# Mask products of an attention kernel on the PE array: eight tiles of 32 rows by 64 columns instead of four of 32 by 128

## The chip, the cores and the metric

The kernel runs on one core of a Trainium2 chip. The metric is the device time of one execution in microseconds (us), lower is better; a kernel's figure is the median over its runs. The profile is one further execution, recorded by the hardware profiler.

## The reference, cut to what matters

Eight sequences (`B = 8`) of 512 positions and 256 features pass through two layers. The first is a feed-forward expert layer whose weights are picked for each sequence by an index. The second is a conditioned transformer layer with 16 heads of 16 features. Only its attention is touched here:

```python
x = _L0_cond_ref(x, itok_B_0_7, ...)                 # gelu(x Wi + bi) Wo + bo + x, then a layernorm
# in the second layer:
scores = jnp.einsum('bhqd,bhkd->bhqk', q / math.sqrt(HEAD_DIM), k)
scores = scores + attention_bias                     # fside, (8, 16, 512, 512), 128 MB
scores = jnp.where(src_mask, -jnp.inf, scores.astype(jnp.float32))
probs = jax.nn.softmax(scores, axis=-1).astype(v.dtype)
ctx = jnp.einsum('bhqk,bhkd->bhqd', probs, v)
# then ctx Wo, a residual, a layernorm, a gelu feed-forward with 1024 hidden features, a residual
```

The mask is a matrix of (8, 1, 512, 512) truth values, the same for all heads.

## The kernel before

**Tiling of the attention.** A step `s` handles one sequence and one block of 32 queries (`QB = 32`), for all 16 heads and all 512 keys; there are 8 x 16 = 128 steps. Heads are held as four quads `u` (`NU = 4`), each on 32 partitions of the q and k tiles, in two halves `r` (`ND = 2`). The scores of a step fill four PSUM tiles, `banks[u]`, each 128 partitions (4 heads x 32 queries) by 512 keys in float32, [...]. There is one set of four, so a step cannot start until the step before has been read out of them.

**A step, engine by engine** (`attention_step`). SP issues the load of the bias block `f` (1 MB, L964) and, every second step, of the mask bytes (L971). POOL turns the mask bytes into bf16 values of 0 or -1e30 in `mh` (L980). PE runs `score`: first the mask products (L990), which copy the mask of 32 queries to the four heads of a bank with a matrix of ones and zeros, `sel`, and open the accumulation (`start=True`), then the score products (L996), which add q k. DVE adds the bias and takes the row maximum (`add`, L1008), POOL negates it (L1021), ACT takes the exponentials (L1029), DVE transposes them in blocks of 32 (L1042).

**Shapes on PE.** The contraction of both products runs over 32 rows. A mask product has a stationary operand of 32 x 128 in bf16 and streams 512 columns; there are 4 in a step, one for each bank. A score product has a stationary operand of 32 x 64 in float32; there are 8 in a step, for each bank the partitions 0 to 63 and 64 to 127. Each float32 product goes to the array in two passes, so the profile counts 16 for a step. Every pass has its own weight load (PEld in the profile).

**Every fourth step** `attend(z)` follows: probabilities times values in 256 products (L1084) with a tile of 64 rows by 32 columns, planned as four pieces of 64 products (`sums`), then 16 small products for the row sums (L1100), the division on DVE, and the output projection (L1124). The names of the other PE lines: L544 is the up projection of either feed-forward layer, L567 the down projection, L716 and L764 are the projections to q, k and v, L522 are transposes, and L918 is the up projection in the last sequence's tail.

**The order of the work** is written out by a planner, `Weave.run`. It holds for each operation an engine, an estimated cost, a key (when it is due) and its dependencies, steps through an estimated time, and emits the operations in that order; each engine then runs its queue strictly in the order emitted, with semaphores between engines. For PE the planner also keeps a stock of instruction words, `words`: an operation's count of instructions, taken from a stock of at most `AT_ONCE = 256.0` that refills at `PER_US = 64.0` a us. An operation whose words are not in stock yet is given a later start. A float32 product counts 4 words (two passes, each a weight load and a product), a bf16 one 2.

Of the kernel before, what the change touches and what calls it, by code (L numbers as in the profile page):

```python
# [12 lines left out]
BF16 = mybir.dt.bfloat16  # L13
# [6 lines left out]
P = 128  # L20
# [6 lines left out]
QB = 32  # L27
# [50 lines left out]
class Weave:  # L78
# [10 lines left out]
    def op(self, engine, cost, key, emit, deps=(), takes=(), uses=(), table=None, lands=0.0,  # L89
           words=0):  # L90
        o = Op()
        o.engine, o.cost, o.key, o.emit = engine, cost, key, emit
        o.takes, o.uses = tuple(takes), tuple(takes) + tuple(uses)
        o.table, o.lands, o.words, o.end, o.done = table, lands, words, None, False
        o.after, o.ready = [], 0.0
        deps = list(deps) + [h.taker for h in uses]
        deps = {id(d): d for d in deps}.values()
        o.waits = len(deps)
        for d in deps:
            d.after.append(o)  # L100
        for h in o.uses:
            h.left += 1
        for h in o.takes:
            h.taker = o
        self.ops.append(o)
        return o
# [79 lines left out]
def tile_expert_ffn_then_conditioned_layer(  # L186
# [36 lines left out]
    nc = tc.nc  # L223
# [4 lines left out]
    ND = D // P  # L228
    NF = FF // P
    NQ = S // QB  # L230
    NU = 4
# [12 lines left out]
    def const(shape, name, dtype=F32):  # L244
        return pool.tile(shape, dtype, name=name)
# [30 lines left out]
    banks = [psum.tile([P, S], F32, name=f"sc_{u}") for u in range(NU)]  # L276
# [22 lines left out]
    eye = cst[:, n_c : n_c + 32]  # L299
    own = cst[:, n_c + 32 : n_c + 64]  # L300

    sel = const([P, 4, QB], "sel", BF16)
    nc.vector.tensor_copy(sel, eye.unsqueeze(1).to_broadcast([P, 4, QB]))

    def tiled(row):
        return row.unsqueeze(1).to_broadcast([P, NT, D])
# [2 lines left out]
    def load(mb, key, emit, **kw):  # L309
        return op("SP", mb / 0.26, key, emit, lands=1.8, **kw)  # L310
# [385 lines left out]
    q_h, k_h, x1t_h, vb_h = ([s.new() for _ in range(B)] for s in (s_q, s_k, s_xt, s_vb))  # L696
# [258 lines left out]
    def attention_step(s):  # L955
        b, i = steps[s]
        z = s // NI
        f, mh, top = s_fs.new(), s_mh.new(), s_top.new()
        if s % NI == 0:
            t_h[z], den_h[z], dg_h[z] = s_t.new(), s_den.new(), s_dg.new()  # L960
        den, t = den_h[z], t_h[z]

        def load_f():
            nc.sync.dma_start(f.tile, fside[b, i].rearrange("h q u k -> (h q) u k"))  # L964

        if s % 2 == 0:
            m8 = before["m8"] = s_m8.new()

            def load_m():
                for h in range(4):  # L970
                    nc.sync.dma_start(  # L971
                        m8.tile[QB * h : QB * h + QB],
                        mask[b, 0, i * QB : (i + 2) * QB, :].rearrange("(i q) k -> q i k", i=2),
                    )

            before["lm"] = load(0.14, s - 2.5, load_m, takes=[m8])
        m8 = before["m8"]

        def convert():
            nc.gpsimd.tensor_scalar(  # L980
                mh.tile, m8.tile[:, s % 2, :].bitcast(U8), MASKED, 1.0, ALU.mult, ALU.mult
            )

        lf = load(1.05, s - 2.4, load_f, takes=[f])
        mc = op("POOL", 0.65, s - 0.7, convert, deps=[before["lm"]], takes=[mh], uses=[m8])

        def score():
            quads = [slice(QB * u, QB * u + QB) for u in range(NU)]
            for u in range(NU):
                nc.tensor.matmul(  # L990
                    banks[u], sel[quads[u]].rearrange("p a q -> p (a q)"), mh.tile[quads[u], :],
                    start=True, stop=False,
                )
            for u in range(NU):
                for r in range(ND):
                    nc.tensor.matmul(  # L996
                        banks[u][64 * r : 64 * r + 64, :], q_h[b].tile[quads[u], r, i, :],
                        k_h[b].tile[quads[u], r, :], start=False, stop=True,
                    )

        sc = op(
            "PE", 1.25, s, score, deps=[mc] + q_ops[b] + k_ops[b] + before.get("A", []),
            uses=[mh, q_h[b], k_h[b]], words=2 * NU + 4 * NU * ND,
        )
        adds = []
        for u in range(NU):
            def add(u=u):
                nc.vector.tensor_tensor_reduce(  # L1008
                    out=f.tile[:, u, :], in0=banks[u], in1=f.tile[:, u, :], scale=1.0,
                    scalar=-3.0e38, op0=ALU.add, op1=ALU.max, accum_out=top.tile[:, u : u + 1],  # L1010
                )

            adds.append(op(
                "DVE", 0.62, s + 0.3, add, deps=[sc, lf], takes=[top] if u == 0 else [],
                uses=[f] + ([top] if u else []),
            ))
        before["A"] = adds

        neg = op(
            "POOL", 0.25, s + 0.3,  # L1020
            lambda: nc.gpsimd.tensor_scalar(  # L1021
                top.tile, top.tile, -BIG, 1.0 / BIG, ALU.mult, ALU.mult
            ),
            deps=adds, uses=[top],
        )
        exps = []
        for u in range(NU):
            def exp(u=u):
                nc.scalar.activation(  # L1029
                    f.tile[:, u, :], f.tile[:, u, :], AF.Exp, bias=top.tile[:, u : u + 1],  # L1030
                    accum_out=den.tile[:, u, s % NI : s % NI + 1],
                )

            first = s % NI == 0 and u == 0
            exps.append(op(
                "ACT", 0.71, s + 1.0, exp, deps=[neg], takes=[den] if first else [],
                uses=[f, top] + ([] if first else [den]), table="exp",
            ))
        E_all.setdefault(z, []).extend(exps)
        for h in range(2):  # L1040
            def turn(h=h):
                nc.vector.transpose(  # L1042
                    t.tile[:, s % NI, 2 * h : 2 * h + 2, :], f.tile[:, 2 * h : 2 * h + 2, :]
                )

            first = s % NI == 0 and h == 0
            T_of.setdefault(z, []).append(op(
                "DVE", 1.23, s + 2.0, turn, deps=exps[2 * h : 2 * h + 2],
                takes=[t] if first else [], uses=[f] + ([] if first else [t]),
            ))  # L1050
        if s % NI == NI - 1:
            attend(z)
# [101 lines left out]
    for b in range(B):  # L1154
        for i in range(NQ):
            if i == 0:
                line_v = values(b)
            attention_step(b * NQ + i)
        nxt = expert_layer(b + 1) if b + 1 < B else ([], [], [])
        ff = feed_forward(b - 1) if b > 0 else ([], [], [])  # L1160
        line = nxt[0] + line_v + ff[0][:2] + nxt[1] + ff[0][2:] + merged(ff[1], nxt[2], 1) + ff[2]
        if b + 1 < B:
            line += projections(b + 1)
        place(line, NQ * b, NQ * (b + 1.0))
# [60 lines left out]
```

## Time and profile before

| | |
|---|---|
| runs of the kernel before | 1056.48, 1062.85, 1064.83 us; median 1062.85 us |
| the profiled execution | 1061.58 us |
| its span, first to last instruction | 1059.8 us (1.8 us lie around it) |
| mean granted PE clock | 0.956 |
| busy: PE, DVE, ACT, POOL | 976.5, 776.6, 681.9, 297.5 us |
| PE products; instructions of all engines | 13329; 32062 |

How to read it: busy time is the union of an engine's instructions. A row of a group gives source line, engine, operation, tiles written and read, shape, count, then busy us, mean ns of one, and the idle time of the engine just before, with what ended it. "issue" means that no semaphore that the profile shows was waited for. A timeline row gives the start in us from the span's start, the length of a merged run of instructions, and how many there were; the length of a run reaches to the end of its last instruction, which on PE overlaps the next one.

### The profile page before, as it was taken

The page shows a single profiled execution, that of the slowest core. Times are in us where ns is not written, and L with a number is a line of the kernel's source. Part 1 is how long each engine was busy: PE and PEld are TensorE (multiplying, and loading weights), DVE is VectorE, ACT ScalarE, POOL GpSimd, SP SyncE. Part 2 cuts the span into 40 slices and gives each one's busy share as a digit, 9 for nine tenths or more (in the row PEclk, how much of TensorE's full clock was granted, in tenths as well). Part 3 has the DMA queues.
Part 4 walks back from the last instruction along what each step waited for, and adds up shares of the span by engine and source line. Part 5 has one row for each costly group of instructions (what it writes and reads, how often), then busy time and mean ns, then how long its engine had stood idle before and what let it go on. Part 6 is the DMA issues. An engine that isn't in the chain of part 4 may idle for free. (4 is left out here: it accounts for less than half of the span.)

```text
span 1059.8 us, 32062 instructions
## 1 busy us (share of the span) xinstructions
PE 976.5 (92%) x13329; PEld 549.1 (52%) x13329; DVE 776.6 (73%) x1837; ACT 681.9 (64%) x1453; POOL 297.5 (28%) x380
## 2 busy tenths in 40 slices
PE   6988989889999998999999999999999999988887
PEld 2643436435546464464745555464645555435466
DVE  1229868877869876789777878789777876777771
ACT  3136684576686755877579585878579574677473
POOL 1241161243222333125232243125132242121110
PEclk9998879989999998999999999999999998899899
DMA  6965436545555544465555645466553434444500
GB/s 202 323 208 173 167 120 230 197 149 190 199 169 194 204 138 147 171 225 181 201 192 190 206 128 199 171 224 181 200 190 130 169 132 146 171 132 163 180 12 17
DMA packets 67591, 183.33 MB, mean 173 GB/s; under 512 B 8212, under 2 KB 46438, under 8 KB 51062
## 3 DMA queue, kind: packets, MB, share of 16 engines
q1 hardware_dynamic: 67158, 181.25, 49.8%
q8 instruction: 104, 1.70, 0.7%
q14 instruction: 41, 0.34, 0.1%
q10 hardware_dynamic: 288, 0.04, 0.0%
HBM read 177.05 MB, written 4.21 MB: 171 GB/s over the span
## 5 line engine op out<-in xcount | busy, mean ns | idle before, releaser
L1029 ACT ACTIVATE fs<-fs,top 128x512 f32<-128x512 f32 x512 | 363.5, 712 | 154.0 <-POOL top L1021 153.0
L1008 DVE CUSTOM_DVE_ANT_0 fs<-sc,fs 128x512 f32<-128x512 f32 x512 | 323.2, 679 | 112.5 <-POOL mh L980 55.5
L1042 DVE STREAM_TRANSPOSE t<-fs 128x1024 f32<-128x1024 f32 x256 | 306.6, 1224 | 55.6 <-PE d L1084 50.3
L1084 PE MATMUL d<-t,vb 64*32 64x128 f32 x8192 | 149.2, 284 | 35.7 <-issue 32.6
L1084 PEld LDWEIGHTS d<-t,vb 64*32 64x32 f32 x8192 | 123.2, 110 | 90.3 <-issue 74.4
L996 PE MATMUL sc<-k,q 32*64 32x512 f32 x2048 | 156.7, 659 | 3.4 <-issue 3.4
L1021 POOL TENSOR_SCALAR top<-top 128x4 f32<-128x4 f32 x128 | 25.7, 201 | 417.8 <-DVE top L1008 368.6
L980 POOL TENSOR_SCALAR mh<-m 128x512 bf16<-128x512 uint8 x128 | 79.1, 618 | 199.5 <-PE sc L990 146.1
L544 PE MATMUL d<-xt,wi 128*128 128x512 f32 x256 | 122.3, 619 | 0.0
L567 PE MATMUL d<-w_t,hid 128*128 128x256 f32 x512 | 119.3, 386 | 2.2 <-issue 2.2
L567 PE MATMUL d<-wo,hid 128*128 128x256 f32 x512 | 120.2, 387 | 0.0
L567 PEld LDWEIGHTS d<-wo,hid 128*128 128x128 f32 x512 | 96.0, 192 | 28.4 <-issue 13.9
L567 PEld LDWEIGHTS d<-w_t,hid 128*128 128x128 f32 x512 | 95.8, 191 | 28.8 <-issue 14.8
L544 PE MATMUL d<-xt,w_t 128*128 128x512 f32 x224 | 105.3, 616 | 0.0
L1029 ACT ACTIVATION_READ_ACCUMULATOR fs<-fs,top 128x1 f32 x512 | 96.1, 188 | 0.0
L990 PE MATMUL sc<-mh,sel 32*128 32x512 bf16 x512 | 71.7, 397 | 19.3 <-DVE top L1008 18.8
L544 PEld LDWEIGHTS d<-xt,wi 128*128 128x128 f32 x256 | 47.5, 195 | 65.1 <-issue 57.7
L647 ACT ACTIVATE hid<-d,bc 128x512 f32<-128x512 f32 x64 | 42.8, 686 | 49.3 <-PE d L544 49.0
L544 PEld LDWEIGHTS d<-xt,w_t 128*128 128x128 f32 x224 | 41.9, 195 | 62.9 <-issue 45.1
L1029 ACT ACT_TABLE_LOAD x50 | 64.2, 1283 | 0.9
L617 POOL TENSOR_TENSOR xn<-xn,rows 128x1024 f32<-128x1024 f32 x24 | 56.7, 2361 | 23.8 <-DMA rows<-in_L_cond_bo_dram 12.5
L996 PEld LDWEIGHTS sc<-k,q 32*64 32x64 f32 x2048 | 31.6, 136 | 50.1 <-issue 49.8
(101 smaller groups left out, 865.6 us busy)
## 6 DMA issues: line engine op xcount, KB each, us to landing
fs<-in_fside_Bx16xSxS_dram SPq DMA_DIRECT2D x128, 1024.0 KB
wi<-in_L_cond_Wi_dram SPq DMA_DIRECT2D x8, 1024.0 KB
wo<-in_L_cond_Wo_dram SPq DMA_DIRECT2D x8, 1024.0 KB
m<-in_mask_Bx1xSxS_bk_dram SPq DMA_DIRECT2D x256, 32.0 KB
xt<-in_x_turned_dram SPq DMA_DIRECT2D x8, 512.0 KB
xn<-in_x_dram SPq DMA_DIRECT2D x8, 512.0 KB
out_dram<-xn SPq DMA_DIRECT2D x32, 128.0 KB
w_t<-in_L_cond_W_dram SPq DMA_DIRECT2D x2, 1024.0 KB
```

What stands on the lines that cost most here:

```text
L544: nc.tensor.matmul(h.tile, wt[:, c, f * P : (f + 1) * P], src.tile[:, c, :], start=(c == 0), stop=(c == ND - 1),)
L567: nc.tensor.matmul(h.tile[:, :D], lhs(f), wt[:, f, :], start=(f == 0), stop=(f == n - 1))
L617: lambda: nc.gpsimd.tensor_tensor(xn[b].tile, xn[b].tile, tiled(row()), alu),
L647: lambda: nc.scalar.activation(hid.tile[:, f, :], h.tile, AF.Gelu, bias=bc[b].tile[:, f : f + 1]),
L980: nc.gpsimd.tensor_scalar(mh.tile, m8.tile[:, s % 2, :].bitcast(U8), MASKED, 1.0, ALU.mult, ALU.mult)
L990: nc.tensor.matmul(banks[u], sel[quads[u]].rearrange("p a q -> p (a q)"), mh.tile[quads[u], :], start=True, stop=False,)
L996: nc.tensor.matmul(banks[u][64 * r : 64 * r + 64, :], q_h[b].tile[quads[u], r, i, :], k_h[b].tile[quads[u], r, :], start=False, stop=True,)
L1008: nc.vector.tensor_tensor_reduce(out=f.tile[:, u, :], in0=banks[u], in1=f.tile[:, u, :], scale=1.0, scalar=-3.0e38, op0=ALU.add, op1=ALU.m ...
L1021: lambda: nc.gpsimd.tensor_scalar(top.tile, top.tile, -BIG, 1.0 / BIG, ALU.mult, ALU.mult),
L1029: nc.scalar.activation(f.tile[:, u, :], f.tile[:, u, :], AF.Exp, bias=top.tile[:, u : u + 1], accum_out=den.tile[:, u, s % NI : s % NI + 1],)
L1042: nc.vector.transpose(t.tile[:, s % NI, 2 * h : 2 * h + 2, :], f.tile[:, 2 * h : 2 * h + 2, :])
L1084: nc.tensor.matmul(pc[r].tile[QB * u : QB * u + QB, :P], vb_h[b].tile[half, j, u, :], t.tile[half, :, u, QB * j : QB * j + QB], start=(j = ...
```

## The change

The mask products of a bank are issued as two products with 64 columns, one for each half `r` of the bank's partitions, in place of one with 128. Tile rows, tile columns and output partitions are then those of the score products that follow. `sel` is cut to 64 columns, and `words` is counted anew: 8 x 2 + 8 x 4 = 48 for a step, where it was 4 x 2 + 8 x 4 = 40. The planner's cost of the operation stays 1.25.

```diff
-    sel = const([P, 4, QB], "sel", BF16)
-    nc.vector.tensor_copy(sel, eye.unsqueeze(1).to_broadcast([P, 4, QB]))
+    sel = const([P, 2, QB], "sel", BF16)
+    nc.vector.tensor_copy(sel, eye.unsqueeze(1).to_broadcast([P, 2, QB]))
...
             for u in range(NU):
-                nc.tensor.matmul(
-                    banks[u], sel[quads[u]].rearrange("p a q -> p (a q)"), mh.tile[quads[u], :],
-                    start=True, stop=False,
-                )
+                for r in range(ND):
+                    nc.tensor.matmul(
+                        banks[u][64 * r : 64 * r + 64, :],
+                        sel[quads[u]].rearrange("p a q -> p (a q)"),
+                        mh.tile[quads[u], :], start=True, stop=False,
+                    )
...
             "PE", 1.25, s, score, deps=[mc] + q_ops[b] + k_ops[b] + before.get("A", []),
-            uses=[mh, q_h[b], k_h[b]], words=2 * NU + 4 * NU * ND,
+            uses=[mh, q_h[b], k_h[b]], words=6 * NU * ND,
```

## The prediction

> **What bounds the kernel now.** I read the page's busy table first, then the stretches, then PE's waits, then one step in the timeline. The page:
>
> ```profile
> PE 976.5 (92%) x13329; PEld 549.1 (52%) x13329; DVE 776.6 (73%) x1837; ACT 681.9 (64%) x1453; POOL 297.5 (28%) x380
> ```
>
> Two of seven equal stretches of 128 us (columns: length; PE, PEld, DVE, ACT, POOL busy us; clock; DMA share; GB/s):
>
> ```profile
> 461.00:589.00 128.00, 124.42 (x1741) 71.40 (x1741) 103.99 (x246) 91.15 (x196) 38.88 (x50) 1.00 0.54 186
> ...
> 845.00:973.00 128.00, 115.26 (x1623) 59.92 (x1622) 93.69 (x216) 85.17 (x181) 34.31 (x46) 0.92 0.42 146
> ```
>
> PE is busy 90 to 97% of every stretch between 77 and 973 us; DVE, the next, 73 to 81%. So time on PE is the time of the kernel, wherever PE isn't held by another. The largest of its waits, without two for the first inputs (9.3 and 4.1 us) and one for `hn` (3.0 us):
>
> ```profile
> PE d L1084 <- issue: 32.6, 22, 3.8
> PE sc L990 <- DVE top L1008: 18.8, 31, 3.2
> ...
> PE sc L996 <- issue: 3.4, 2, 2.4
> PE d L1084 <- DVE bc L636: 3.1, 3, 1.0
> ...
> PE d L567 <- issue: 2.2, 1, 2.2
> ```
>
> Two things hold PE. First, 38.2 us in 25 waits on "issue", all but three in the dense L1084 products. Going through the records one by one, the places lie 256 PE instructions, or multiples of it, apart: PE runs out of fetched instructions. Second, 18.8 us in which a mask product waits for DVE to empty its bank; these fall in 16 of the 128 steps.
>
> Now one step, PE's timeline:
>
> ```profile
> 504.44 0.55 PE L1084 MATMUL d<-t,vb 64*32 64x128 f32 x20
> 504.92 0.40 PE L990 MATMUL sc<-mh,sel 32*128 32x512 bf16 x4
> 505.25 1.11 PE L996 MATMUL sc<-k,q 32*64 32x512 f32 x16
> 506.29 0.34 PE L1084 MATMUL d<-t,vb 64*32 64x128 f32 x8
> ```
>
> Masks to scores takes 0.325 us, scores to the next line 1.044 us: these are also the medians over all steps (101 and 107 of the 128 lie within 0.016 us). Five float32 products of the full array just before show what a change of tile costs:
>
> ```profile
> 499.31 2.31 PE L544 MATMUL d<-xt,w_t 128*128 128x512 f32 x5
> 501.55 0.40 PE L1084 MATMUL d<-t,vb 64*32 64x128 f32 x2
> ```
>
> Their starts lie 0.427 us apart; 501.55 - 499.31 = 2.24 = 5 x 0.427 + 0.10. The 0.10 appears at each change of tile shape (L996 to L567: 0.517 from the last start, 0.090 over; L567 to L990: 0.312, 0.099 over 0.213), and not between L544 and L567, same shape (0.429).
>
> [...] The float32 loads agree: 102, 127 and 186 ns for the first of 32, 64 and 128 columns, some 0.8 ns a column. [...] The mask's load of 128 columns shows 90 ns, below the 32-column one, so it is fast now [...]. [...] The trace has the blocks (104 packets, 1.70 MB on queue q8) [...].
>
> **The change part by part.** *PE, one step.* Now, split so that it adds up:
> - masks 0.325 = starts of four spread over 0.010, one bf16 pass 0.213 (half of 0.427), drain and the fast load 0.102.
> - scores 1.044 = first weight load 0.053, two passes 2 x 0.427, starts of eight spread over 0.047, drain 0.090. The second passes' loads are hidden: they stand in the records under the first passes, and the second pass starts 0.480 = 0.427 + 0.053 after the first.
>
> Together 1.369 us. After, the mask is a third pass of the same eight tiles: weight load 0.053 [...], 0.213, 2 x 0.427, twice 0.007 handing over (last start of one pass to first start of the next is 0.434 now), 0.047 of spread, drain 0.090: 1.271. Saved 0.098, taken as 0.10. That rests on the drain between masks and scores going, and on the score weights loading under the masks.
>
> Bounds for the unseen:
> - The mask's load is still fast (0.013, an estimate from 90 against 102 ns at 32 columns): saved 0.138.
> - The score weights can't load under bf16 passes: saved 0.045.
> - The drain stays, since bf16 to float32 also drains (the trace has no other change of type to tell it by): masks 0.053 + 0.213 + 0.047 + 0.090 = 0.403 for 0.325: lost 0.078.
>
> *What counts on the path.* 128 steps, less those where another limit takes the gain. Of the 25 fetch waits, 13 follow a 256-instruction block that holds a whole step; there the block merely waits longer for its instructions. In the 16 steps with a DVE wait I count half: the adds that mask waits for themselves start after the scores of the step before, which come earlier too, as long as DVE isn't behind. 128 - 13 - 8 = 107; 107 x 0.10 = 10.7 us. What is late next at the other steps is PE's own following work (L567, L544, L1084), ready in 92% of the time.
>
> *Instructions.* 4 more products and 4 more loads a step, 1024 in all: four more blocks on 104. At 38.2 us for 104, +1.5 us. Issue itself is hidden: eight loads and products start 0.0067 us apart, in the 0.047 above. A mask product with its wait has the same things queued behind it as before.
>
> *The planner.* `words` 48 for 40 moves starts. Comparing the two orders: 35 of some 600 runs of equal PE work differ; about once a sequence from the third on, a mask-and-score operation stands one or two L567 halves earlier, once the transposes of `hn` are interleaved with `sums`, and in the tail L567 and `sums` alternate. DVE follows in 35 places (adds before transposes), ACT in 27, POOL in 5 with the same instructions. On SP the same loads are issued, in 17 places three `fs` loads in a row or a `rows` load earlier; `fs` has five buffers and DMA is busy 42 to 54%, so I take that as hidden; if not, it costs about one wait like the DVE ones, 1 us a sequence. Earlier masks can meet a full bank (a wait of 0.6 to 1 us, as in the DVE row) but also start DVE earlier. I take 0, bounds -4 and +6.
>
> The block boundaries also fall elsewhere. Counting the new order in 256s with the durations above, blocks that would run in under 4.5 us are 34, as before; 13 for 14 under 2.5 us. So the number of waits should stay; which ones are long is chance: a wait is 0.2 to 3.8 us, mean 1.5, so 25 of them give about +-6 us with their spread.
>
> *`sel` copy*: one DVE instruction of half the size in the start, 0.
>
> Sum: 1061.6 (the profiled execution, 1.3 below the median of 1062.85) - 10.7 + 1.5 = **1052.4**, rounded to 1052.
>
> **The rivals.** A measurement of this kernel can tell about 1%, 10.6 us, from no change.
> - *Better than that*: mask weights load fast, so 107 x 0.138 = 14.8 less, + 1.5: 1048.3. [...] Chance 0.14.
> - *Score weights aren't hidden*: 107 x 0.045 = 4.8 less, + 1.5: 1058.3. For it: no load of one type under products of another is in the trace. Against: the passes of L996 do just that with one type. Chance 0.11.
> - *Fetch and order eat it*: PE drains the same instructions faster and asks for 4% more, so the waits grow by 6 us more and the order costs 4: 1052.4 + 10 = 1062. For it: the waits are 38 us already, and none but chance decides their place. Against: dense blocks are as many as before. Chance 0.12.
> - *Slower: the drain stays.* One mechanism, at each change from mask to scores: [...] eight starts plus an unhidden, slower load come on top: 0.078 x 107 = 8.3, + 1.5: 1071.4; it is slower than before as soon as the drain left is above 0.02 us. The same sign, if the two columns' tiles of a row group can't stream bf16 side by side at full rate: 0.213 more, less the 0.098, 0.115 lost a step, 1075.4. For it: nothing in the trace separates type from shape. Against: [...] float32 tiles of this shape do stream side by side (eight passes in 0.48 us). Chance 0.13.
> - That the change doesn't do what it says: the order shows eight mask products of 64 columns in each step, so no.
>
> **How the numbers follow.** The forecast case has 0.50. Its own range is 1045 to 1059 (fetch and order +-6, joined), with a little under half of it below 1051. Faster by over 1%: 0.24 of it, 0.14 of the better case, 0.03 of the others: 0.41. Slower by over 1%: of the drain case 0.09, of fetch and order 0.02: 0.11. Within: 0.48. The range for 8 in 10 runs from 1044 (the better case with luckier fetches; some 0.06 lie below) to 1067 (above the fetch rival and below most of the drain case; some 0.11 lie above).
>
> **What would show it.** Right: the masks' first start to the scores' first start falls from 0.325 to about 0.27 us and scores to next line from 1.044 to about 1.00; the score product's median duration falls below 638 ns, since its first pass no longer waits for its weights; PE's busy time falls by 11 to 14 us; "issue" waits stay at 38 +- 6 us. Wrong: masks to scores at 0.40 or more (drain or half rate); scores to next line still 1.044 (weights not hidden); PE's busy time down but its waits on "issue" or on DVE up by as much (fetch and order).

## The result, and the profile after

Measured side by side, the kernel before took 1063.06 us (median of 4) and the changed one 1050.14 us (median of 4): 12.9 us less, a ratio of 0.989 with a 95% interval of 0.984 to 0.994. Measured again later it was 0.988 (0.984 to 0.993). The forecast was 1052 us, the range 1044 to 1067. Single runs of one kernel lie up to 1.5% apart, so differences under some 5 us between medians of a few runs are not read below. A profile is one such run: what it says of the whole span has that uncertainty too, what it says of a step, as a median over 128, has not.

The profiled execution has a span of 1047.8 us against 1059.8, 12.0 less. The page:

```profile
PE 959.5 (92%) x13841; PEld 560.5 (53%) x13841; DVE 774.9 (74%) x1837; ACT 681.5 (65%) x1453; POOL 298.1 (28%) x380
```

PE is busy 17.0 us less, DVE as long as before; 512 products were added (13329 to 13841). The same two stretches as ahead, in the same columns (length; PE, PEld, DVE, ACT, POOL busy us; clock; DMA share; GB/s):

```profile
461.00:589.00 128.00, 122.50 (x1895) 71.20 (x1896) 101.58 (x240) 90.75 (x196) 38.34 (x49) 0.99 0.50 176
...
845.00:973.00 128.00, 113.58 (x1913) 65.03 (x1912) 97.51 (x226) 88.35 (x195) 31.70 (x48) 0.94 0.46 160
```

PE is still the engine without slack, 89 to 96% of these stretches. One step, in PE's timeline:

```profile
509.70 3.18 PE L567 MATMUL d<-w_t,hid 128*128 128x256 f32 x14
512.82 0.42 PE L991 MATMUL sc<-mh,sel 32*64 32x512 bf16 x8
513.06 1.04 PE L998 MATMUL sc<-k,q 32*64 32x512 f32 x16
514.03 0.48 PE L567 MATMUL d<-w_t,hid 128*128 128x256 f32 x1
```

Masks to scores is 0.240 us (it was 0.325), scores to the next line 0.970 (1.044); both are the medians over all steps. Together 1.210 for 1.369: **0.159 us a step**, where 0.098 was forecast. All instructions of the mask line and of the score line (duration in ns: least, median, most):

```profile
L991 PEld LDWEIGHTS <-sel x1024: 101/101/124, 79.0 to 1003.0; 32*64 32x64 bf16 x171
L991 PE MATMUL sc<-mh,sel x1024: 371/398/631, 79.0 to 1003.0; 32*64 32x512 bf16 x171
...
L998 PE MATMUL sc<-k,q x2048: 584/587/1112, 79.2 to 1003.7; 32*64 32x512 f32 x187
```

and the score line before:

```profile
L996 PE MATMUL sc<-k,q x2048: 584/638/1111, 78.1 to 1020.8; 32*64 32x512 f32 x187
```

The median score product takes 587 ns, which was 638. In the records the products of the first pass were the long ones, 638 ns where the second pass showed 587; now both passes show 587. In the step above the score weights begin to load at 512.84 us, under the mask products and 0.22 ahead of the first score product at 513.06; in the prediction's step of the kernel before, the first load and the first score product both start at 505.25. PE's waits:

```profile
PE d L1086 <- issue: 29.5, 16, 3.6
PE sc L991 <- DVE top L1010: 17.4, 32, 3.1
...
PE d L1086 <- DVE bc L636: 5.2, 3, 1.7
PE sc L991 <- issue: 4.2, 3, 2.4
...
PE d L1086 <- ACT hid L924: 2.9, 1, 2.9
PE d L544 <- ACT xt L827: 2.1, 5, 0.9
...
PE sc L998 <- issue: 2.0, 1, 2.0
```

"issue" sums to 35.7 us in 20 waits, from 38.2 in 25. The waits for `bc`, `hid` and `xt` (the latter two of ACT) are longer than before or new. Those for `hid` stand in the tail, after the last step:

```profile
1003.16 1.13 PE L998 MATMUL sc<-k,q 32*64 32x512 f32 x16
1004.22 3.72 PE L918 MATMUL d<-xt,w_t 128*128 128x256 f32 x16
1009.59 1.99 PE L918 MATMUL d<-xt,w_t 128*128 128x256 f32 x8 [1.64 <-ACT hid L924]
1012.23 0.41 PE L893 MATMUL d<-ident,hn 128*128 128x128 f32 x2 [0.65 <-DVE hn L868]
1012.48 1.89 PE L567 MATMUL d<-w_t,hid 128*128 128x256 f32 x8
1017.31 1.49 PE L1086 MATMUL d<-t,vb 64*32 64x128 f32 x64 [2.94 <-ACT hid L924]
1018.73 1.99 PE L567 MATMUL d<-w_t,hid 128*128 128x256 f32 x8
1020.65 1.16 PE L1086 MATMUL d<-t,vb 64*32 64x128 f32 x64
```

Before, from the chain of work that ended last:

```profile
1027.00 6.91 PE d L567 x32
1033.91 2.60 PE d L1084 x175
```

Now L567 and the sums (L1086) alternate, where they stood one after the other, and PE waits for ACT twice. The last step starts at 1002.9 us, 16.3 earlier than before (1019.2), but the tail after it is 44.9 us long for 40.6. So 16.3 us were gained in the main loop and 4.3 given back in the tail.

**The sum by kind.** For each kind of work I take every interval from one PE start to the next, less idle time, and count time in the windows whose granted clock is 0.5 (94.8 us of them in the profile before, 98.9 after) as half: in the profile before, starts of L567 lie 427 ns apart in such windows and 216 outside. The steps' own work falls by 19.5 us. Half-clock time lands less on steps and more on L567: +1.9 net. Other work +0.5, idle +4.9. Sum -12.2, the span's 12.0. In 93 of the 128 steps neither profile has a wait inside (a gap over 20 ns between products) or half clock; there the median gain is 0.159 us, 14.3 in all. The 22 steps with a wait on DVE inside gained 2.9.

### The profile page after: what moved, and what is told of

Read it like the earlier page. It is cut to its first block, busy times and chain, and to the rows that moved or that the text cites. A ratio compares the mean times of both kernels' runs of the same rounds, so it can differ in the third digit from the quotient of the medians.

```text
span 1047.8 us, 33083 instructions
## 1 busy us (share of the span) xinstructions
PE 959.5 (92%) x13841; PEld 560.5 (53%) x13841; DVE 774.9 (74%) x1837; ACT 681.5 (65%) x1453; POOL 298.1 (28%) x380
## 5 line engine op out<-in xcount | busy, mean ns | idle before, releaser
L1010 DVE CUSTOM_DVE_ANT_0 fs<-sc,fs 128x512 f32<-128x512 f32 x512 | 322.1, 679 | 98.9 <-PE sc L998 51.1
L1086 PE MATMUL d<-t,vb 64*32 64x128 f32 x8192 | 151.1, 287 | 38.4 <-issue 29.5
L1086 PEld LDWEIGHTS d<-t,vb 64*32 64x32 f32 x8192 | 125.1, 111 | 91.3 <-issue 67.0
L998 PE MATMUL sc<-k,q 32*64 32x512 f32 x2048 | 149.6, 627 | 2.0 <-issue 2.0
L567 PE MATMUL d<-wo,hid 128*128 128x256 f32 x512 | 123.0, 394 | 0.0
L544 PE MATMUL d<-xt,wi 128*128 128x512 f32 x256 | 122.8, 621 | 0.0
L567 PE MATMUL d<-w_t,hid 128*128 128x256 f32 x512 | 122.2, 391 | 0.0
L567 PEld LDWEIGHTS d<-wo,hid 128*128 128x128 f32 x512 | 97.9, 195 | 33.1 <-issue 18.0
L567 PEld LDWEIGHTS d<-w_t,hid 128*128 128x128 f32 x512 | 97.0, 194 | 27.7 <-issue 13.6
L544 PE MATMUL d<-xt,w_t 128*128 128x512 f32 x224 | 105.2, 616 | 2.1 <-ACT xt L827 2.1
L991 PE MATMUL sc<-mh,sel 32*64 32x512 bf16 x1024 | 76.5, 412 | 21.7 <-DVE top L1010 17.4
L544 PEld LDWEIGHTS d<-xt,wi 128*128 128x128 f32 x256 | 47.6, 195 | 65.3 <-issue 56.1
L544 PEld LDWEIGHTS d<-xt,w_t 128*128 128x128 f32 x224 | 41.6, 194 | 60.9 <-issue 42.5
L991 PEld LDWEIGHTS <-sel 32*64 32x64 bf16 x1024 | 21.4, 102 | 97.6 <-issue 53.3
```

Source lines behind the costliest of these rows:

```text
L544: nc.tensor.matmul(h.tile, wt[:, c, f * P : (f + 1) * P], src.tile[:, c, :], start=(c == 0), stop=(c == ND - 1),)
L567: nc.tensor.matmul(h.tile[:, :D], lhs(f), wt[:, f, :], start=(f == 0), stop=(f == n - 1))
L991: nc.tensor.matmul(banks[u][64 * r : 64 * r + 64, :], sel[quads[u]].rearrange("p a q -> p (a q)"), mh.tile[quads[u], :], start=True, stop= ...
L998: nc.tensor.matmul(banks[u][64 * r : 64 * r + 64, :], q_h[b].tile[quads[u], r, i, :], k_h[b].tile[quads[u], r, :], start=False, stop=True,)
L1010: nc.vector.tensor_tensor_reduce(out=f.tile[:, u, :], in0=banks[u], in1=f.tile[:, u, :], scale=1.0, scalar=-3.0e38, op0=ALU.add, op1=ALU.m ...
L1086: nc.tensor.matmul(pc[r].tile[QB * u : QB * u + QB, :P], vb_h[b].tile[half, j, u, :], t.tile[half, :, u, QB * j : QB * j + QB], start=(j = ...
```

## The experiments

Three questions: is it the shape or the operand type whose change costs the 0.10 us between masks and scores; what did the new order do; and how much is owed to the place where the blocks of 256 instructions fall? Two theories: A, the step's gain reaches the end but for waits on DVE, and the new order costs its tail; B, the main loop was helped by luck of order and blocks. In the table, "last" is the start of the last step in the profile, "half clock" the sum of the windows with a granted clock of 0.5; ratio to the kernel before with its interval. Each ratio is to the kernel before as measured beside it: its medians were 1063.06 us (the changed kernel), 1061.96 (the next four rows), 1062.79 (t32, shift64, shift128, stock128) and 1060.52 (the rest). Medians from different groups, which ran on different chips, are therefore compared by their ratios too.

| kernel | median us (runs) | ratio | span | last | tail | issue waits | half clock |
|---|---|---|---|---|---|---|---|
| before | 1063.06 (4) | | 1059.8 | 1019.2 | 40.6 | 38.2 | 94.8 |
| changed | 1050.14 (4) | 0.989 (0.984-0.994) | 1047.8 | 1002.9 | 44.9 | 35.7 | 98.9 |
| again: the changed kernel | 1047.42 (6) | 0.988 (0.984-0.993) | 1044.9 | 998.5 | 46.5 | 32.7 | 101.6 |
| w40: new tiles, old order | 1045.53 (6) | 0.986 (0.980-0.991) | 1043.9 | 1001.7 | 42.1 | 40.9 | 88.7 |
| b48: old tiles, new order | 1059.96 (14) | 0.999 (0.996-1.002) | 1060.6 | 1014.2 | 46.4 | 33.5 | 98.6 |
| nomask | 1037.43 (4) | 0.977 (0.972-0.982) | 1035.6 | 989.1 | 46.5 | 40.1 | 98.0 |
| t32 | 1081.88 (4) | 1.018 (1.012-1.024) | 1080.1 | 1033.6 | 46.5 | 42.1 | 111.7 |
| shift64 | 1067.09 (20) | 1.004 (1.001-1.006) | 1070.3 | 1022.6 | 47.7 | 44.3 | 116.1 |
| shift128 | 1050.34 (4) | 0.989 (0.982-0.996) | 1047.9 | 1001.4 | 46.5 | 36.7 | 94.9 |
| shift192 | 1062.55 (20) | 1.002 (0.999-1.004) | 1067.3 | 1020.8 | 46.5 | 41.6 | 111.4 |
| b_shift64 | 1070.05 (4) | 1.010 (1.005-1.016) | 1067.1 | 1027.1 | 40.1 | 41.8 | 95.6 |
| b_shift128 | 1067.63 (20) | 1.006 (1.004-1.008) | 1068.7 | 1029.1 | 39.7 | 37.8 | 111.7 |
| stock128: new tiles | 1035.95 (4) | 0.977 (0.970-0.983) | 1034.5 | 984.9 | 49.5 | 10.7 | 84.5 |
| b_stock128: old tiles | 1048.74 (4) | 0.989 (0.984-0.995) | 1046.8 | 997.3 | 49.5 | 6.1 | 81.7 |

**Shape or type.** What the prediction calls the drain is the 0.09 to 0.10 us that the profile before shows at the changes of tile shape between L544, L567, L990, L996 and L1084; what the array does in that time the trace does not show. Between masks and scores both the shape and the type changed in the kernel before; in the changed kernel only the type does. With the mask in sixteen tiles of 32 x 32 both change again:

```diff
-                for r in range(ND):
+                for h in range(4):
                     nc.tensor.matmul(
-                        banks[u][64 * r : 64 * r + 64, :],
-                        sel[quads[u]].rearrange("p a q -> p (a q)"),
+                        banks[u][QB * h : QB * h + QB, :], sel[quads[u], 0, :],
                         mh.tile[quads[u], :], start=True, stop=False,
```

> The mask products in sixteen tiles of 32 x 32, still bf16, in the order of the changed kernel. A tile shape that the scores don't have: [...] If the shape (theory A): masks to scores 0.013 (load of 32 columns) + 0.213 + 0.050 (starts of sixteen, 0.0033 apart) + 0.09 = 0.37 us, scores to next line back at 1.044 or 1.02, so the step is near 1.39 and the kernel about as slow as before, ratio 0.998 to 1.006. If narrow tiles as such are what pays and the drain never mattered, masks to scores stays under 0.28 and the ratio near 0.988.

Its timeline:

```profile
526.04 0.43 PE L991 MATMUL sc<-mh,sel 32*32 32x512 bf16 x16
526.41 1.11 PE L997 MATMUL sc<-k,q 32*64 32x512 f32 x16
527.45 0.48 PE L567 MATMUL d<-w_t,hid 128*128 128x256 f32 x1
```

0.365 and 1.044, which are the medians too: scores to the next line as before, masks to scores near the 0.37 expected if it is the shape. From the last mask start to the first score start the records show 0.315 us, as before, against 0.217 with 32 x 64, where one pass is 0.213 (an estimate, half of the 0.427 between two-pass float32 products). Both change from bf16 to float32, only one changes shape: the shape costs about 0.10. For the type there is at most the 0.027 by which a tile's mask pass exceeds 0.213 in the changed kernel; at the 0.44 ns a column that the bf16 loads show (101 ns for 64 columns, 87 for 32) a load of 64 columns would come to about that, 0.028 (an estimate). The step is 0.040 longer than before (5 us over 128), yet the kernel is 19 us slower: 1.018, where 0.998 to 1.006 was expected. It issues 64 instructions a step where the planner counts 48; issue waits and half-clock time are up by 3.9 and 16.9 us. By the sum by kind the 20.3 us between the spans are 6.0 of the steps' own work, 6.3 of half clock and 8.1 of idle time. Why the last two grew was not tested apart.

**The order alone.** In w40 the new tiles keep the old count of words, in b48 the old tiles have the new one. The edit of b48 (that of w40 is its reverse, in the changed kernel):

```diff
-            uses=[mh, q_h[b], k_h[b]], words=6 * NU * ND,
+            uses=[mh, q_h[b], k_h[b]], words=2 * NU + 4 * NU * ND,
```

> The changed kernel once more, on the chip that runs the next three. In its profile the step takes 0.240 + 0.970 us where it took 0.325 + 1.044, 0.159 less, 20.4 us over 128 steps; the span fell by 12.0. Theory A (the step's gain reaches the path nearly whole, and the new order of the tail gives 4.3 us back): ratio to before 0.988 +- 0.003, last mask product near 1003 us, then 45 us of tail. Theory B (the main loop was helped by where the instruction blocks happened to fall): the same ratio on average, but the place of the last mask product moves by several us from one profile to the next.

> The new tiles with the old count of words, 40, so that the planner writes the order of before. Theory A: step as in the changed kernel (0.240 and 0.970 us), tail after the last mask product back at 40.6 us from 44.9; span about 1043.5, ratio to before 0.983 to 0.985. Theory B (the new order itself helped the main loop): the main loop loses what the order gave, and the kernel is no faster than the changed one: ratio 0.988 to 0.994.

> The old tiles with the new count of words, 48, so that the planner writes the order of the changed kernel. Theory A: step as before (0.325 and 1.044 us), tail near 45 us, so about 4 us slower than before: ratio 1.002 to 1.006. Theory B: the main loop gains from the order, ratio under 0.998.

The changed kernel once more has the same ratio, but its last step starts 4.4 us earlier and its tail is 1.6 longer: single profiles of one kernel differ by that much. Theory A's tail is there: 46.4 us with old tiles in the new order, 42.1 with new tiles in the old. But b48 is not 4 us slower. Its last step starts 5.0 us earlier than before, with 33.5 us of issue waits for 38.2, and the kernel ends level (0.999, by 14 runs and 19). So each theory is half right: with the new order the main loop gained about what the tail lost. Whether the order itself gave that, or the places where the blocks then fall, these runs don't tell. The tiles alone, with the order held, are worth 16.4 us between the medians in the old order (1061.96 for the kernel before in that comparison, to w40) and 9.8 to 12.5 in the new (b48 to the two medians of the changed kernel). w40 and the changed kernel can't be told apart.

**How much of PE's time arrives.** All mask products left out, `start=True` at the scores:

```diff
-            for u in range(NU):
-                for r in range(ND):
-                    nc.tensor.matmul(
-                        banks[u][64 * r : 64 * r + 64, :],
-                        sel[quads[u]].rearrange("p a q -> p (a q)"),
-                        mh.tile[quads[u], :], start=True, stop=False,
-                    )
...
-                        k_h[b].tile[quads[u], r, :], start=False, stop=True,
+                        k_h[b].tile[quads[u], r, :], start=True, stop=True,
```

> The changed kernel, same order, without any mask product: the mask is left out of the scores, the score products open the accumulation. It measures how much of the time taken from PE in each step reaches the end. A step loses 0.240 us and its first score weights (0.053 us for 0.027) are no longer hidden: 0.21 us less, 27 us over 128 steps. If three quarters arrive, as theory A has it for the main loop (16.3 of 20.4 us), the span falls from 1047.8 by some 20 us to 1028, ratio to before 0.968 to 0.973. If DVE takes over as the bound, it falls by less than 13 us: ratio above 0.976.

```profile
505.20 1.11 PE L991 MATMUL sc<-k,q 32*64 32x512 f32 x16
506.25 3.72 PE L567 MATMUL d<-w_t,hid 128*128 128x256 f32 x16
```

A step is now the 1.044 us of the scores alone (L991 is their line here): 0.166 less than in the changed kernel, not 0.21, since the unhidden weights also spread the eight starts over 0.047 again. Of 0.166 x 128 = 21.2 us, 10.0 arrive between the medians (12.2 and 9.3 between the spans). The wait on issue grew to 40.1 us. So only about half of what is taken from each step reached the end here, and the expectation of three quarters was wrong. The ratio of 0.977 is that of the other case, DVE as the bound, but PE's waits on `top` of DVE are not longer (14.9 us for 17.4); what grew is the wait on issue.

**The blocks of 256 instructions.** More small transposes at the start, two instructions each, move every boundary through the work, with the order unchanged (32 more for the shift by 64, 64 and 96 more for 128 and 192):

```diff
-        nc.tensor.transpose(h_col.tile[:, :at], br_t, ident[:at, :at])
+        for _ in range(33):
+            nc.tensor.transpose(h_col.tile[:, :at], br_t, ident[:at, :at])
```

> The changed kernel with 32 more of the first small transposes (L422), 64 instructions ahead of everything that matters, so that each boundary between blocks of 256 instructions falls 64 instructions earlier in the work. If the places of the boundaries are luck of several us: issue waits at other places, their sum different from 35.6 us by 3 to 8 us in either direction, and the time with it. If the place doesn't matter: same sum within 2 us and ratio to before 0.988 +- 0.004. The added transposes stand in the start, where PE waits for loads, and cost up to 3 us.

> The same with 64 more transposes, boundaries 128 instructions earlier; up to 6 us in the start. Luck of the boundaries: issue waits differ from both others by 3 to 8 us. No luck: the same sum within 2 us.

> The changed kernel with 96 more transposes, boundaries 192 instructions earlier. The shifts 0, 64 and 128 gave 1047 to 1050, 1067 and 1050 us. If the place decides by chance: anywhere from 1045 to 1068, with issue waits and half-clock time low or high together with it; if the shift by 64 was slow for another reason (the added transposes themselves), this one is slower still, above 1070.

> The kernel before with 32 more small transposes at the start, boundaries between blocks of 256 instructions 64 instructions earlier. The changed kernel lost 17 to 20 us by this. If the luck of the boundaries belongs to any order: the sum of issue waits and the time move by up to 15 us in either direction (ratio 0.985 to 1.015). If only the changed kernel is sensitive: ratio 1.000 +- 0.003.

> The same with 64 more transposes, 128 instructions earlier. Same alternatives. With the three shifts of the changed kernel these give the gain of the tiles as a mean over places: theory A has it at 12 to 17 us.

The luck is larger than I had it. With the boundaries 64 instructions earlier the changed kernel takes 1067 us, with 128 earlier 1050, with 192 earlier 1063. The first step starts 0.8, 4.3 and 7.4 us later than in the changed kernel, so up to 7 us of these are the transposes; the rest isn't. The profiled executions of the shifts by 64 and 192 are the slowest of their 20 runs, 5.0 and 6.5 us above the medians. PE's waits in the shift by 64:

```profile
PE d L1087 <- issue: 30.5, 18, 3.4
PE sc L992 <- DVE top L1011: 16.9, 30, 3.1
...
PE sc L999 <- issue: 8.5, 3, 3.6
```

With smaller entries, issue is 44.3 us in 25 waits, 8.6 more than in the changed kernel. Half-clock time is up by 17.2 us, which costs half of that in work, 8.6. These two make 17.2 of the 22.5 us between the spans. The kernel before moves too, in both shifts upwards (1.010, 1.006); but of the 7.1 us in the shift by 128 the transposes can be 5.7, since its first step starts that much later. As a mean over the three places that both have, the changed kernel is faster by (12.9 + 3.0 + 17.3) / 3 = 11 us between the medians; at the place 64 it is 3 us. The pairs at 64 and 128 come from two chips; by the ratios they are 7.0 and 18.6, and the mean 13.

The sum by kind, taken for each pair of old and new tiles at one place, tells the steady part from the rest. The steps' own work falls by 19.4 us at the old place, by 17.0 at 64, by 19.5 at 128: PE gains much the same at each place. Half-clock and idle time together take 6.9 us of it at the old place and 19.1 at 64, and give 2.9 more at 128.

**Fetch made easy.** The planner's stock halved, so that it spreads the dense sums; once with the new tiles, once with the old, which there have the new count of words, 48, so that both have one order:

```diff
-    AT_ONCE, PER_US = 256.0, 64.0
+    AT_ONCE, PER_US = 128.0, 64.0
```

> The changed kernel with AT_ONCE = 128.0 for 256.0 in the planner, so that it spreads the dense L1084 products. If the fetch of instructions is what the gain partly runs into: the blocks that run in under 3 us become rarer, issue waits fall from 35.6 to 15 to 22 us, changes of tile shape rise by some 50 (50 x 0.15 = 7.5 us more), net 6 to 12 us faster than the changed kernel: ratio to before 0.977 to 0.983. If the waits on issue aren't fetch, they stay near 35 us and the kernel is slower than the changed one by the 7.5 us: ratio 0.995.

> The old tiles, four of 32 x 128, in the order of the run stock128 (AT_ONCE = 128.0, 48 words), which has few fetch waits (10.7 us). It shows what the new tiles are worth when instruction fetch hardly interferes. Theory A (the step's 0.159 us reach the path but for the waits on DVE): 14 to 19 us slower than stock128, 1050 to 1055, ratio to before 0.988 to 0.993, issue waits still near 10 us. Theory B (what the new tiles seemed to bring is mostly luck of the blocks): within 8 us of stock128, ratio under 0.985.

The 0.15 us for a change of tile shape in the first of these was my estimate; the profile before shows 0.09 to 0.10 for the change, and 0.053 where a float32 load of 64 columns isn't hidden. First, waits of the new tiles (stock128):

```profile
PE sc L991 <- DVE top L1010: 23.0, 35, 3.7
...
PE d L1086 <- DVE t L1044: 6.2, 2, 5.8
...
PE sc L998 <- issue: 3.3, 2, 2.3
```

then of the old tiles in the same order (b_stock128):

```profile
PE sc L990 <- DVE top L1008: 24.6, 38, 3.7
...
PE d L1084 <- DVE t L1042: 6.2, 2, 5.8
PE d L1084 <- issue: 4.5, 5, 1.9
```

Issue waits fall to 10.7 and 6.1 us, as they should if PE waits there for instructions. The trace speaks for that: in the kernel before, all 25 stand at one place modulo 256 in PE's instructions (to within one), and each ends 1.2 to 1.6 us after the end of a 16 KB packet on q8, the queue that the profile names "instruction"; the 20 of the changed kernel stand at the same place, 1.2 to 1.5 us after such a packet. DVE now heads PE's waits. Order, tail and waits on DVE are alike in the pair, and the new tiles are faster by 12.8 us (1048.74 to 1035.95; 13.7 by the ratios, as the pair comes from two chips; spans 12.3). That is the cleanest figure for them. Of the pair's steps 102 are free of waits and at full clock; they gain 15.9 us, 0.159 in the median. The other 26 lose 1.4, so the steps' own work falls by 14.5; other work gains 0.5, half clock and idle time take 1.3 each back: issue 4.6 more, other waits less. Theory A had 14 to 19 us, theory B at most 8 between the two; what was found lies at A's lower edge.

stock128 beats both kernels of this study, at 0.977 of before.

## Why the prediction was right, and where it wasn't

- **The mechanism: right.** The 0.10 us between masks and scores go (0.217 from the last mask start, for a pass of 0.213; 0.315 again in t32), and the score weights load under the masks (score products 587 ns, second pass 0.429 after the first, where it was 0.480). The trace of before showed what a change of shape costs, 0.09 to 0.10 us, and loads hidden in float32 alone. That a change of type costs nothing of the kind no row of it could show; this was a bet, and it held (at most 0.027 us are left, see t32). Of the signs named, issue waits came as said (35.7 us); PE's busy time fell by 17.0 us, where 11 to 14 were named, because the step gained more.
- **The step: 0.159 us where the sum said 0.098**, beyond its upper bound of 0.138. The place is the line of the sum "weight load 0.053 ..., twice 0.007 handing over, 0.047 of spread". By the records the first mask pass holds the array 0.027 longer than a pass, not 0.053: the 0.053 is what this trace shows for the float32 loads of 64 columns, and as an estimate for bf16 it was twice too long. The load of 64 bf16 columns shows 101 ns, the one of 128 before it 91. The working had called the latter fast against a float32 load of 32 columns, 102 ns; in bf16 that load shows 87 (t32). Starts are spread over 0.023, not 0.047, since they come 0.0033 apart; handing over is about 0.004 and 0.002. The spread of 0.047 belonged to the unhidden float32 load that goes, not to the eight tiles.
- **The share that arrives: too high.** "107 x", 84% of 128 steps. With the true 0.159 this gives 17.0 us; the pair with few issue waits shows 12.8, 63% of 20.4. What the sum left out stands above: in that pair the 26 steps with a wait or half clock gain nothing in their own work, and waits and half clock grow by 2.6 us. The two errors, of opposite sign, cancel in 1052: that the forecast came within 2 us of 1050 is luck.
- **Fetch: +1.5 forecast.** -2.5 in the changed kernel's profile, +4.6 in the stock pair. So blocks that are as many and as dense did not fix the sum, and "+-6 us" for the place of the blocks was too narrow: shifts of 64 moved one kernel by up to 17 us. I left out that a wait can be followed by half-clock time (last section). The rival "fetch and order eat it" is thus not dead: at another place of the blocks it would have been the result.
- **The order at 0: right as a sum**, from 5.0 us gained in the main loop and 5.8 lost in the tail at old tiles (b48). The tail was named, its price was not, and that the two cancel was not forecast.
- **The rival "the drain stays"** fell with the profile of the changed kernel; t32, where the shape changes too, has the 0.10 us back (0.315 where the changed kernel has 0.217).

## What to carry to other kernels

Give small products that follow each other one tile shape, even if this doubles their number: a change of shape cost 0.09 to 0.10 us here, and the next weights hid only behind products of the same shape. Take the median of the step from the trace, multiply by the number of steps, and expect only a part of it at the end when other waits are near: here some 60% on average, but from 15% to 85% in single pairs (3.0 and 17.3 of 20.4 us). Where PE waits on "issue" at distances of 256 instructions, a gain or loss of 1% between two kernels may be the place of the blocks (a shift by 64 instructions made the changed kernel 17 us slower here); shift the program by some instructions and measure again before believing it.

## What the runs showed of the hardware that was not expected

- A load of 64 bf16 columns is worth 0.027 us of array time (from a tile's mask start to its score start 0.240, less a pass of 0.213, itself an estimate: half of the 0.427 between two-pass float32 products), 0.42 ns a column; of 64 float32 columns 0.053 (0.480 less 0.427), 0.83 ns a column. The loads agree: in bf16 those of 64 and 32 columns show 101 and 87 ns (t32), 0.44 ns for each column more.
- Starts of products in one phase come 3.3 ns apart when the loads are bf16, or under bf16 products as in the changed kernel's scores, and 6.7 ns when float32 loads are exposed; the second pass, its weights loaded ahead, keeps the distance of the first.
- Places that differ by 64 instructions in a program of some 27700 for PE change the time by 17 us, with an identical order. At the 25 waits of the kernel before, PE goes on with the next 256 instructions 3.2 to 6.4 us after it entered the 256 before them, and where sums (L1084) follow each other without a gap, PE takes 1.8 us for 256 instructions.
- With each of its seven waits of 2.2 us and more on instructions the profile before shows half clock, in windows of 3.4 or 6.8 us that begin late in the wait or up to 1.5 us after it: at 290.95 us PE resumes after 2.45 us and the half clock runs from 291 on. In the shift by 64 it is seven of ten. With the clock at 0.5 a window of 3.4 us does 1.7 us less work, so a wait of 2.5 us can cost some 4 (an estimate from these numbers). These windows are 31 of the 95 us at half clock in the profile before; the others were not traced to a cause.
